# The GRU gates of a graph layer as seven block products of 384 columns instead of 256, with two products added in place

## The chip, the cores and the metric

The kernel runs on one core of a Trainium2 chip. The metric is the device time of one execution in microseconds (us), taken as the median of several runs. A separate profiled execution gives the trace from which all durations of instructions come. The engines are named as in the profile: PE is TensorE (matmul), PEld its weight load, DVE VectorE, ACT ScalarE, POOL GpSimd, SP SyncE (which here only issues DMAs).

## The reference

64 graphs of 256 nodes with 256 features go through two layers, each followed by a residual and a LayerNorm. Layer 0 is a normalised adjacency product and a linear layer. Layer 1 has a convolution over the nodes with 17 taps (branch `x_conv`), a message branch (`x_nmp`), and then a GRU cell, which is what the change touches:

```python
x_in = jnp.concatenate([x_conv, x_nmp], axis=-1)
gi = x_in @ w_ih.T + b_ih
gh = x @ w_hh.T + b_hh
r = jax.nn.sigmoid(gi_r + gh_r)
z = jax.nn.sigmoid(gi_z + gh_z)
nn_ = jnp.tanh(gi_n + r * gh_n)
return (1.0 - z) * nn_ + z * x
...
x = _layernorm(x + _L1_gnn_ref(...), axis=-1)
```

`gi` has 768 columns (r, z, n) from 512 inputs, `gh` 768 columns from 256. r and z need only the sum of both parts; n needs its two parts apart, because r multiplies one of them. Everything is fp32.

## The kernel before

**Stages.** The 64 graphs are taken in four quarters of 16 (`Q`, `NQ`). `graphs` (L960) makes layer 0 and the first pieces of layer 1 for a graph; its result for the gates goes out to memory as `xn` (x transposed, and the message branch). The convolution is done in the frequency domain for a whole quarter at once: `products` (L557) multiplies by the transformed weights in twelve steps, `complex_end` (L731) transforms back on VectorE and writes `xc_d`. Then `gru` (L832) computes the gates of one graph. The main loop (L1056) mixes these generators:

- four graphs of each of the first three quarters have their gates early, among the layer pieces of the last graphs of the next quarter (`gates(q, range(EARLY))`, L1094);
- the other twelve wait (`late`, L1101) and are mixed with the next quarter's `products` and then with its `complex_end`; `paced` (L942) hands out pieces of `complex_end` at a rate per marked VectorE operation of the gates (`mark`, L91; `RATES`, L1042);
- in the last quarter the late gates of the third lie beside `complex_end` alone (L1086), and its own 16 graphs of gates stand at the end with nothing beside them (L1103).

**Order.** Program order is made by these generators (each `yield` is a place where another may put a piece in). When the kernel is built, a planner fixes one order for each engine, by program order among the instructions that it expects to be ready. On the chip each engine executes its fixed order.

**Banks.** Matmul results of `products` and of `gru` go to four PSUM banks (`accbank`, L85), used in turn; a bank is given out again when its last reader is done. Each holds 512 fp32 columns.

**The gates of a graph.** `inputs` holds six chunks of 128 input rows by 256 nodes: chunks 0 and 1 are x, 2 and 3 the message branch, 4 and 5 the convolution branch, which `transposed` (L800) puts there. r and z are made from a 2 by 2 blocking: three chunks by three, 128 nodes by 128 nodes (`halves`, L818), and r columns by z columns. In Strassen's way (Winograd's form) seven block products take the place of eight. Their left sides are A11, A12, A22 and four sums S made by GpSimd (`input_sums`, L822), their right sides B11, B21, B22 and four differences T of weights, made once (L997). Each block product is three matmuls of 256 columns (`block`, L844); `first` (L859), L860, L865, L866 and L869 put the seven together on VectorE, L868 and L870 make tanh of half the value (sigmoid).

n is then made directly: for each half of the nodes six matmuls of 256 columns, two for the x part and four for the rest, into the two halves of one bank (L883). L888 to L908 add the bias, multiply by r, add, take tanh, and mix with x. LayerNorm (L313) and an output DMA follow, on `x1_g`, of which there are two buffers.

A trace shows each fp32 matmul as two PE records, so a graph has 42 records in L846 and 24 in L883.

Of the kernel before, what the change touches and what calls it, by code (L numbers as in the profile page):

```python
# [14 lines left out]
P = 128  # L15
# [11 lines left out]
def kernel(  # L27
# [93 lines left out]
    vectors = const.tile([16, P], F32, name="bn_in")  # L121
# [29 lines left out]
    wrz = const.tile([P, 7, HALF, D], F32)  # L151
    B11, B21, B22, T1, T2, T3, T4 = range(7)
    wn = const.tile([P, 3 * DCH, D], F32)
    brz_t = const.tile([P, 2, D], F32)
    bn_t = const.tile([P, 2, D], F32)
# [266 lines left out]
    def x1_transposed(g):  # L422
        x1 = X1.pop(g)
        xn = XN[g] = work.tile([P, 2 * DCH, N], F32, name="xn")
        p = bank("p_x1T").rearrange("p (k n) -> p k n", k=DCH)
        for k in range(DCH):
            for c in range(NCH):
                nc.tensor.transpose(p[:, k, c * P : (c + 1) * P], x1[:, c, k * P : (k + 1) * P], ident)
        nc.scalar.copy(xn[:, :DCH], p)  # L429

    def layer1(g, place):
# [4 lines left out]
        x1T = xn[:, :DCH]  # L436
# [80 lines left out]
        nc.scalar.copy(xn[:, DCH:], p)  # L517
# [115 lines left out]
    def turned(re, im, angle):  # L633


        t = freq.tile([P, 2, D], F32, name="turn", bufs=3)
        x, y = M[:, re, :], M[:, im, :]
        real_part(t[:, int(re > im), :], x, y, angle)
        return imaginary_part(t[:, int(re < im), :], x, y, angle), t
# [4 lines left out]
    def real_transform():  # L644


        sub2(M[:, 0:3:2, :], M[:, 1:4:2, :])
        yield

        sub2(M[:, 4:6, :].rearrange("p a o -> p (a o)"), M[:, 6:8, :].rearrange("p a o -> p (a o)"))  # L650
        add2(M[:, 6, :], M[:, 7, :])
        r = math.sqrt(0.5)
        for i, by in enumerate((-1.0, 1.0, -r, r)):
            stt(M[:, 4 + i, :], M[:, 4 + i, :], by, M[:, i, :], op0=ALU.mult, op1=ALU.add)
        stt(M[:, 0:4, :], M[:, 0:4, :], 2.0, M[:, 4:8, :], op0=ALU.mult, op1=ALU.subtract)
        yield

        run(four(8, 12))
        yield
        nc.vector.tensor_sub(M[:, 8, :], M[:, 0, :], M[:, 8, :])  # L660
        nc.vector.tensor_add(M[:, 12, :], M[:, 4, :], M[:, 12, :])
        for i, x, y in ((1, 9, 13), (2, 10, 14), (3, 15, 11)):
            angle = math.pi * ORDER[i] / 8
            t = freq.tile([P, 2, D], F32, name="turn", bufs=3)
            by = real_part(t[:, 0, :], M[:, x, :], M[:, y, :], angle)
            imaginary_part(t[:, 1, :], M[:, x, :], M[:, y, :], angle)
            stt(M[:, 8 + i, :], t[:, 0, :], -by, M[:, i, :], op0=ALU.mult, op1=ALU.add)
            stt(M[:, 12 + i, :], t[:, 1, :], by, M[:, 4 + i, :], op0=ALU.mult, op1=ALU.add)
            yield
        stt(M[:, 0:8, :], M[:, 0:8, :], 2.0, M[:, 8:16, :], op0=ALU.mult, op1=ALU.subtract)  # L670
        yield
# [43 lines left out]
    def output(q, n, re, im):  # L715
# [4 lines left out]
        t = freq.tile([P, 2, D], F32, name="turn", bufs=3)  # L720
# [79 lines left out]
    def transposed(g):  # L800
# [3 lines left out]
        if in_blocks(g):  # L804
            behind(nc.vector.transpose(xcT.rearrange("p k (s r) -> p k s r", r=RB), CONV.pop(g)))
            nc.gpsimd.tensor_tensor(xcT, xcT, inputs[:, :DCH], op=ALU.add)
            for k in range(DCH):
                nc.scalar.activation(xcT[:, k], xcT[:, k], AF.Relu, bias=bn2_bias[:, k : k + 1])  # L808
            return
# [12 lines left out]
    def input_sums(g):  # L822
        A11, A12, A21, A22 = halves(GATE[g][1])
        S = SUMS[g] = gate.tile([P, 4, HALF, P], F32, name="sums", bufs=1)
        nc.gpsimd.tensor_tensor(S[:, 0], A21, A22, op=ALU.add)  # L825
        second = nc.gpsimd.tensor_tensor(S[:, 1], S[:, 0], A11, op=ALU.subtract)  # L826

        with tc.issue_after(second.ins):
            nc.gpsimd.tensor_tensor(S[:, 2], A11, A21, op=ALU.subtract)
            nc.gpsimd.tensor_tensor(S[:, 3], A12, S[:, 1], op=ALU.subtract)  # L830

    def gru(g):  # L832
# [5 lines left out]
        trz = gate.tile([P, 4, D], F32, name="trz", bufs=1)  # L838
        nn = gate.tile([P, NCH, D], F32, name="nn", bufs=1)
# [4 lines left out]
        def block(p, j, a, b):  # L844
            for k in range(HALF):
                nc.tensor.matmul(  # L846
                    p[:, j * D : (j + 1) * D], a[:, k], wrz[:, b, k], start=k == 0, stop=k == HALF - 1
                )

        p15, p26 = accbank("p_rz"), accbank("p_rz")  # L850
        block(p15, 0, A11, B11)
        block(p26, 0, A12, B21)
        block(p15, 1, S[:, 0], T1)
        block(p26, 1, S[:, 1], T2)
# [3 lines left out]
        first = gate.tile([P, 2, D], F32, name="first", tag="gn")  # L858
        mark(nc.vector.tensor_add(first, half(p15), brz_t), 1)  # L859
        nc.vector.tensor_add(trz[:, 0:2], first[:, 0:1].to_broadcast([P, 2, D]), half(p26))  # L860
        p7, p34 = accbank("p_rz"), accbank("p_rz")
        block(p7, 0, S[:, 2], T3)
        block(p34, 0, S[:, 3], B22)
        block(p34, 1, A22, T4)
        nc.vector.tensor_add(trz[:, 3], trz[:, 1], p7[:, :D])  # L865
        mark(nc.vector.tensor_add(trz[:, 1:3], trz[:, 1:4:2], half(p34)), 1)  # L866

        nc.scalar.activation(trz[:, 0:4:2], trz[:, 0:4:2], AF.Tanh, scale=0.5)  # L868
        nc.vector.tensor_add(trz[:, 1:4:2], trz[:, 1:4:2], first[:, 1:2].to_broadcast([P, 2, D]))  # L869
        nc.scalar.activation(trz[:, 1:4:2], trz[:, 1:4:2], AF.Tanh, scale=0.5)  # L870
# [3 lines left out]
        for c in range(NCH):  # L874
            terms = [(inputs[:, k, c * P : (c + 1) * P], wn[:, k]) for k in range(3 * DCH)]
            if c == 0 and following:
                input_sums(g + 1)
            if c == 1 and g % Q + 2 < Q:
                load_conv(g + 2)
            p = accbank("p_n")  # L880
            for o, part in ((1, terms[:DCH]), (0, terms[DCH:])):
                for j, (lhsT, w) in enumerate(part):
                    nc.tensor.matmul(  # L883
                        p[:, o * D : (o + 1) * D], lhsT, w, start=j == 0, stop=j == len(part) - 1
                    )

            gn = gate.tile([P, 2, D], F32, name="gn")
            mark(nc.vector.tensor_add(gn, p.rearrange("p (i d) -> p i d", i=2), bn_t), 1)  # L888
            nc.vector.scalar_tensor_tensor(
                gn[:, 1, :], trz[:, 2 * c], 1.0, gn[:, 1, :], op0=ALU.add, op1=ALU.mult  # L890
            )
            nc.vector.scalar_tensor_tensor(  # L892
                gn[:, 0, :], gn[:, 1, :], 0.5, gn[:, 0, :], op0=ALU.mult, op1=ALU.add
            )
            nc.scalar.activation(nn[:, c, :], gn[:, 0, :], AF.Tanh)  # L895


            if g == B - 1:
                part = slice(c, c + 1)
            elif c == NCH - 1:  # L900
                part = slice(0, NCH)
            else:
                yield
                continue
            y, t, n = x1[:, part], trz[:, 1:4:2][:, part], nn[:, part]
            mark(nc.vector.scalar_tensor_tensor(y, t, 3.0, y, op0=ALU.add, op1=ALU.mult), 1)
            nc.vector.scalar_tensor_tensor(n, t, 1.0, n, op0=ALU.subtract, op1=ALU.mult)
            nc.vector.tensor_sub(y, y, n)  # L908
            layernorm(y, nc.scalar, 4 * LN_EPS)
            nc.scalar.dma_start(out[g].rearrange("(c p) d -> p c d", p=P)[:, part], y)  # L910
            yield
# [61 lines left out]
    with tc.tile_pool(name="setup", bufs=1) as setup:  # L973
# [10 lines left out]
        def gate_weights():  # L984
            for b, half_inputs, cols in ((B11, 0, 0), (T1, 0, 1), (B21, 1, 0), (B22, 1, 1)):
                at = slice(cols * D, (cols + 1) * D)
                if half_inputs == 0:
                    parts = ((slice(0, DCH), w_hhT), (slice(DCH, HALF), w_ihT[D : D + P]))
                else:
                    parts = ((slice(0, 1), w_ihT[D + P :]), (slice(1, HALF), w_ihT[:D]))  # L990
                for k, w in parts:
                    nc.sync.dma_start(wrz[:, b, k], w[:, at].rearrange("(k p) o -> p k o", p=P))
            for k, w in ((0, w_hhT), (DCH, w_ihT[D:]), (2 * DCH, w_ihT[:D])):
                nc.sync.dma_start(wn[:, k : k + DCH], w[:, 2 * D :].rearrange("(k p) o -> p k o", p=P))
            yield

            for to, a, b in ((T3, B22, T1), (T1, T1, B11), (T2, B22, T1), (T4, B21, T2)):  # L997
                with tc.issue_after(marks[-1][0]):
                    nc.vector.tensor_sub(wrz[:, to], wrz[:, a], wrz[:, b])
# [10 lines left out]
        brz = brz_t.rearrange("p i d -> p (i d)")  # L1010
        nc.vector.tensor_add(brz, bih_t[:, : 2 * D], bhh_t[:, : 2 * D])
        nc.vector.tensor_sub(brz_t[:, 1], brz_t[:, 1], brz_t[:, 0])
        nc.vector.tensor_copy(bn_t[:, 0, :], bih_t[:, 2 * D :])
        nc.vector.tensor_copy(bn_t[:, 1, :], bhh_t[:, 2 * D :])
# [143 lines left out]
```

## Time and profile before

| what | value |
|---|---|
| median of 3 runs | 2149.64 us (2147.59 to 2150.93) |
| the profiled execution, first to last instruction | 2152.3 us |
| granted TensorE clock, mean | 0.990 of full |
| PE records in L883 (n) | 1536, 355.1 us busy |
| PE records in L846 (r, z) | 2688, 348.6 + 271.6 us busy |
| VectorE at L859 to L869 (5 operations a graph) | 42.9 + 43.6 + 26.5 + 43.9 + 64.6 us |
| VectorE at L888, L889, L892 (twice a graph) | 87.3 + 69.9 + 69.8 us |
| GpSimd at L825 to L830 (4 sums a graph) | 67.1 + 72.6 + 79.6 + 79.9 us |

The span of the profiled execution lies 2.7 us above the median of the runs. Busy time of PE is the union of its records; records overlap (each lasts about 380 ns, one starts every 216 ns), so a sum of durations says nothing.

### The profile page before, as it was taken

What the parts mean: (1) busy time and instruction counts of PE and PEld (TensorE: products, weight loads), DVE (VectorE), ACT (ScalarE), POOL (GpSimd) and SP (SyncE); (2) the same over time, 40 slices, a digit from 0 to 9 for tenths busy, and PEclk for the clock granted to TensorE, in tenths of its full rate; (3) what the DMA queues carried; (4) which work ended last, traced back from release to release, by engine and by line L of the source; (5) the groups of instructions that cost most, each with busy time, mean ns of one, the idle gap of its engine ahead of it and who ended that gap; (6) DMA issues with size and microseconds to landing.
All of it is one profiled execution on the core that took longest, in us unless ns stands there. A gap on an engine that the chain in (4) does not pass through costs nothing.

```text
span 2152.3 us, 28977 instructions
## 1 busy us (share of the span) xinstructions
PE 2052.7 (95%) x9693; PEld 1735.8 (81%) x9693; DVE 1581.6 (73%) x3719; ACT 841.9 (39%) x1857; POOL 664.8 (31%) x640
## 2 busy tenths in 40 slices
PE   7999999887999999899999999999999998999997
PEld 5888788776888888788888888777888887788886
DVE  5555578775568788775656988876566889988887
ACT  4665643456431123445552122446553112222222
POOL 2444310121431244213322133323231123444442
PEclk9999999999999999999999999999999999999999
DMA  4766666434346644233326654324324744443331
GB/s 122 235 196 197 198 194 207 142 132 134 96 146 203 203 110 128 93 112 113 113 94 190 205 157 113 118 98 133 102 88 136 243 116 122 119 102 99 94 84 54
DMA packets 295085, 298.30 MB, mean 139 GB/s; under 512 B 76414, under 2 KB 273618, under 8 KB 294938
## 3 DMA queue, kind: packets, MB, share of 16 engines
q1 hardware_dynamic: 235050, 200.46, 30.9%
q10 hardware_dynamic: 44480, 67.39, 8.8%
q0 software_dynamic: 15408, 28.61, 6.1%
q8 instruction: 77, 1.26, 0.2%
q14 instruction: 70, 0.57, 0.1%
HBM read 193.28 MB, written 103.06 MB: 138 GB/s over the span
## 4 chain that ended last, share of the span: by engine, by line
PE 44%; DVE 12%; issue 9%; POOL 6%; ACT 4%; DMA 2%; ACTq 0%; SPq 0%; POOLq 0%; DVEq 0%
PE p_rz L846 14%; PE p_n L883 8%; PE p_k L539 7%; PE p_out L409 2%; PE p_nmp L513 2%; PE p_hT L399 2%; PE p_dft L480 2%; POOL ln_rs L323 2%; PE p_conv L443 1%; PE p_msg L464 1%; PE p_dist L504 1%; POOL sums L826 1%; POOL sums L825 1%; DMA u<-ud 1%; POOL xc_g L796 1%
## 5 line engine op out<-in xcount | busy, mean ns | idle before, releaser
L883 PE MATMUL p_n<-wn,inputs 128*128 128x256 f32 x1536 | 355.1, 385 | 13.4 <-DVE first L859 13.2
L846 PE MATMUL p_rz<-wrz,sums 128*128 128x256 f32 x1536 | 348.6, 380 | 1.3 <-DVE gn L888 0.8
L883 PEld LDWEIGHTS p_n<-wn,inputs 128*128 128x128 f32 x1536 | 288.5, 192 | 64.2 <-DVE first L859 20.9
L846 PEld LDWEIGHTS p_rz<-wrz,sums 128*128 128x128 f32 x1536 | 290.0, 190 | 44.5 <-issue 5.2
L846 PE MATMUL p_rz<-wrz,inputs 128*128 128x256 f32 x1152 | 271.6, 379 | 1.0 <-ACT inputs L808 1.0
L323 POOL TENSOR_TENSOR ln_rs<-ln_rs,neg_half 128x2 f32<-128x2 f32 x129 | 99.1, 768 | 510.9 <-DVE ln_rs L322 464.0
L846 PEld LDWEIGHTS p_rz<-wrz,inputs 128*128 128x128 f32 x1152 | 217.6, 190 | 31.1 <-ACT inputs L808 1.2
L895 ACT ACTIVATE nn<-gn 128x256 f32<-128x256 f32 x128 | 53.3, 417 | 332.1 <-DVE gn L892 331.7
L539 PE MATMUL p_k<-u,VM 128*128 128x256 f32 x736 | 175.2, 380 | 2.7 <-DMA u<-ud 1.9
L369 POOL TENSOR_TENSOR dis<-deg,neg_half 128x2 f32<-128x2 f32 x64 | 46.1, 720 | 423.6 <-DVE deg L367 393.1
L333 ACT ACTIVATE x_g<-x_g,ln_mr,ln_rs 128x256 f32<-128x256 f32 x128 | 70.0, 593 | 241.5 <-DVE ln_mr L331 241.5
L539 PEld LDWEIGHTS p_k<-u,VM 128*128 128x128 f32 x736 | 138.1, 190 | 24.4 <-DMA u<-ud 4.1
L480 PE MATMUL p_dft<-fwd,h 128*128 128x240 f32 x512 | 120.2, 379 | 25.9 <-ACT h L447 24.6
L399 PE MATMUL p_hT<-adjT,x 128*128 128x256 f32 x512 | 129.8, 397 | 14.0 <-DVE adjT L381 7.6
L825 POOL TENSOR_TENSOR sums<-inputs 128x384 f32<-128x384 f32 x64 | 67.1, 1048 | 239.0 <-ACT inputs L816 206.3
L480 PEld LDWEIGHTS p_dft<-fwd,h 128*128 128x128 f32 x512 | 95.2, 192 | 47.6 <-ACT h L447 41.2
L506 DVE TENSOR_TENSOR aT<-aT,adjT 128x512 f32<-128x512 f32 x64 | 44.6, 698 | 118.2 <-ACT aT L505 118.1
L443 PE MATMUL p_conv<-wc,xn 128*128 128x259 f32 x512 | 125.8, 388 | 4.3 <-ACT xn L429 4.3
L392 POOL TENSOR_TENSOR x_t<-x_t,b_t 128x512 f32<-128x512 f32 x64 | 85.4, 1334 | 142.6 <-ACT x L391 97.4
L409 PE MATMUL p_out<-w,hT 128*128 128x256 f32 x512 | 123.1, 383 | 1.4 <-ACT hT L404 0.7
L464 PE MATMUL p_msg<-wmsg,xn 128*128 128x256 f32 x512 | 121.4, 380 | 0.0
L513 PE MATMUL p_nmp<-aT,msg 128*128 128x256 f32 x512 | 121.2, 379 | 0.2 <-DVE aT L506 0.2
(157 smaller groups left out, 3910.2 us busy)
## 6 DMA issues: line engine op xcount, KB each, us to landing
u<-ud SPq DMA_DIRECT2D x284, 256.0 KB
xn_d<-xn ACTq DMA_DIRECT2D x64, 512.0 KB
inputs<-xn_d SPq DMA_DIRECT2D x64, 512.0 KB
ud<-u_set POOLq DMA_DIRECT2D x39, 480.0 KB, 6.1
adj_t<-in_adj_dram SPq DMA_DIRECT2D x64, 256.0 KB
x_t<-in_x_dram SPq DMA_DIRECT2D x64, 256.0 KB
x_d<-x ACTq DMA_DIRECT2D x64, 256.0 KB
xc_d<-VM SPq DMA_DIRECT2D x64, 256.0 KB
```

The costliest lines, as they stand in the source:

```text
L323: nc.gpsimd.tensor_tensor(rs[:, : len(chunks)], rs[:, : len(chunks)], neg_half[:, : len(chunks)], op=ALU.pow)
L392: nc.gpsimd.tensor_tensor(x_t, x_t, b0_t.unsqueeze(1).to_broadcast([P, NCH, D]), op=ALU.add)
L399: nc.tensor.matmul(p[:, k, :], x1[:, mc, k * P : (k + 1) * P], adjT[:, mc, 1 - mc : 3 - mc, :].rearrange("p n q -> p (n q)"), start=mc == ...
L409: nc.tensor.matmul(p[:, c, :], hT[:, k, c * P : (c + 1) * P], w0[:, k, :], start=k == 0, stop=k == DCH - 1)
L443: nc.tensor.matmul(p, x1T[:, k, c * P : (c + 1) * P], wc1[:, k, :], start=k == 0, stop=k == DCH - 1)
L464: nc.tensor.matmul(p[:, c, :], x1T[:, k, c * P : (c + 1) * P], wmsg[:, k, :], start=k == 0, stop=k == DCH - 1)
L480: nc.tensor.matmul(p[:, t0 * FL : t1 * FL], h[:, c, k * P : (k + 1) * P], fwd[:, first : first + t1 - t0, :].rearrange("p t f -> p (t f)") ...
L513: nc.tensor.matmul(p[:, k, :], msg[:, mc, k * P : (k + 1) * P], aT[:, mc].rearrange("p n q -> p (n q)"), start=mc == 0, stop=mc == NCH - 1,)
L539: nc.tensor.matmul(p[:, j * D : (j + 1) * D], v[:, k, :], u[:, k, :], start=k == 0, stop=k == DCH - 1)
L825: nc.gpsimd.tensor_tensor(S[:, 0], A21, A22, op=ALU.add)
L846: nc.tensor.matmul(p[:, j * D : (j + 1) * D], a[:, k], wrz[:, b, k], start=k == 0, stop=k == HALF - 1)
L883: nc.tensor.matmul(p[:, o * D : (o + 1) * D], lhsT, w, start=j == 0, stop=j == len(part) - 1)
```

## The change

All of r, z, and both parts of n go through the seven block products. The output columns are split in halves of 128 (`HD`) instead of in r and z, and each half has four kinds of columns: n from x (`GN`), r, z, and n from the other inputs (`GI`), 512 columns in one bank. The input chunks are reordered so that each half of the inputs has one chunk of x and two others. The x chunk feeds GN, GR and GZ, the other two chunks GR, GZ and GI, so each matmul has 384 columns, and one block product (three matmuls) fills one bank. Two of the seven products, S3·B22 and A22·T4, are added by TensorE onto the banks of S0·T1 (`p5`) and S2·T3 (`p7`) after VectorE has read those for another sum; VectorE then reads the banks again. `G` takes the place of `trz`, `nn`, `gn` and `first`. One sum (the bias of the second column half) is made by GpSimd. The last elementwise steps work on all 512 values of a kind at once.

```diff
+    ball = const.tile([P, 2, 4, D // 2], F32)
+    vectors = ball[:16, 0, 0, :]
...
-    wrz = const.tile([P, 7, HALF, D], F32)
+    HD = D // 2
+    GN, GR, GZ, GI = range(4)
+    wall = const.tile([P, 7, HALF, 3, HD], F32)
-    wn = const.tile([P, 3 * DCH, D], F32)
-    brz_t = const.tile([P, 2, D], F32)
-    bn_t = const.tile([P, 2, D], F32)
...
-        nc.scalar.copy(xn[:, :DCH], p)
+        nc.scalar.copy(xn[:, 0 : 2 * DCH : 2 * DCH - 1], p)
...
-        nc.scalar.copy(xn[:, DCH:], p)
+        nc.scalar.copy(xn[:, 1 : 1 + DCH], p)
...
-        t = freq.tile([P, 2, D], F32, name="turn", bufs=3)
+        t = freq.tile([P, 2, D], F32, name="turn", bufs=2)
...
+    def input_sums(g, which=(0, 1, 2, 3)):
         A11, A12, A21, A22 = halves(GATE[g][1])
-        S = SUMS[g] = gate.tile([P, 4, HALF, P], F32, name="sums", bufs=1)
...
+        S = SUMS.setdefault(g, [])
+        for i in which:
+            S.append(gate.tile([P, HALF, P], F32, name=f"sums{i}", bufs=1))
+            x, y, op = ((A21, A22, ALU.add), (S[0], A11, ALU.subtract), (A11, A21, ALU.subtract), (A12, S[1 % len(S)], ALU.subtract))[i]
+            nc.gpsimd.tensor_tensor(S[i], x, y, op=op)
...
+        G = gate.tile([P, NCH, 2, 4, HD], F32, name="G", bufs=1)
...
+        def product(a, b, p=None):
+            first = p is None
+            if first:
+                p = accbank("p_g")
             for k in range(HALF):
                 nc.tensor.matmul(
+                    p[:, : 3 * HD] if k == 0 else p[:, HD:], a[:, k], wall[:, b, k].rearrange("p t d -> p (t d)"),
+                    start=first and k == 0, stop=True, skip_group_check=not first or k > 0,
+                )
+            return p
...
+        p1 = product(A11, B11)
+        p2 = product(A12, B21)
+        p6 = product(S[1], T2)
         yield
         if following:
             sent(g + 1)
+        mark(nc.vector.tensor_add(quarter(0, 0), p1, bias(0)), 1)
+        nc.vector.tensor_add(quarter(1, 0), quarter(0, 0), p6)
+        nc.gpsimd.tensor_tensor(quarter(0, 1), quarter(1, 0), bias(1), op=ALU.add)
+        nc.vector.tensor_add(quarter(0, 0), quarter(0, 0), p2)
+        p5 = product(S[0], T1)
+        p7 = product(S[2], T3)
+        mark(nc.vector.tensor_add(quarter(1, 1), quarter(0, 1), p5), 1)
         if following:
             transposed(g + 1)
         yield
+        product(S[3], B22, p5)
+        mark(nc.vector.tensor_add(quarter(1, 1), quarter(1, 1), p7), 1)
+        if following:
+            input_sums(g + 1)
+        yield
+        product(A22, T4, p7)
+        nc.vector.tensor_add(quarter(0, 1), quarter(0, 1), p5)
+        mark(nc.vector.tensor_add(quarter(1, 0), quarter(1, 0), p7), 1)
...
+            nc.scalar.activation(
+                both[:, :, GR : GZ + 1, :].rearrange("p q t d -> p q (t d)"),
+                both[:, :, GR : GZ + 1, :].rearrange("p q t d -> p q (t d)"), AF.Tanh, scale=0.5,
             )
+            nc.vector.scalar_tensor_tensor(n, r, 1.0, n, op0=ALU.add, op1=ALU.mult)
+            nc.vector.scalar_tensor_tensor(i, n, 0.5, i, op0=ALU.mult, op1=ALU.add)
+            nc.scalar.activation(i, i, AF.Tanh)
...
+            mark(nc.vector.scalar_tensor_tensor(yq, z, 3.0, yq, op0=ALU.add, op1=ALU.mult), 1)
+            nc.vector.scalar_tensor_tensor(i, z, 1.0, i, op0=ALU.subtract, op1=ALU.mult)
+            nc.vector.tensor_sub(yq, yq, i)
```

In the text below q00, q10, q01 and q11 are the four quarters of `G` (node half, column half), with the operation that writes them named after them. The weights are loaded by 16 DMAs in place of 11 (rows of 128 columns in place of 256), and the four differences of weights are 1152 columns wide instead of 768.

## The prediction

> **What bounds the kernel now.** I read the page first, then busy time by stage, then the timeline of TensorE and VectorE in two stages, then the waits. In these windows the columns are length, PE, PEld, DVE, ACT and POOL busy us (with instructions), granted clock, DMA share and GB/s.
>
> ```profile
> PE 2052.7 (95%) x9693; PEld 1735.8 (81%) x9693; DVE 1581.6 (73%) x3719; ACT 841.9 (39%) x1857; POOL 664.8 (31%) x640
> ...
> 536.00:642.00 106.00, 102.25 (x486) 86.73 (x484) 64.80 (x164) 43.26 (x96) 43.87 (x42) 1.00 0.40 117
> 642.00:755.00 113.00, 112.57 (x530) 99.02 (x531) 90.70 (x169) 19.73 (x39) 22.99 (x21) 1.00 0.69 206
> 755.00:960.00 205.00, 194.55 (x916) 163.94 (x915) 168.38 (x397) 78.77 (x175) 63.80 (x60) 0.98 0.38 111
> 960.00:1148.00 188.00, 185.46 (x905) 155.57 (x904) 112.69 (x302) 100.59 (x232) 61.25 (x62) 1.00 0.36 108
> ...
> 1740.00:1905.00 165.00, 153.66 (x710) 132.01 (x709) 155.79 (x322) 37.68 (x79) 66.55 (x58) 0.99 0.43 117
> 1905.00:2152.00 247.00, 235.86 (x1080) 203.96 (x1080) 201.51 (x363) 69.66 (x136) 102.46 (x98) 0.99 0.30 83
> ```
>
> TensorE is 95% busy overall, but the stages differ. From the starts of `first` (L859, once per graph) and the program, the 64 gate graphs fall into five kinds of place. A: 12 lie among layer-0 and layer-1 pieces (536:642, 960:1148, 1470:1655), TensorE full, VectorE near 60%. B: 10 lie among the convolution's products (642:755 and its two repeats), TensorE full, VectorE about 80%. C: 16 lie beside `complex_end` and layer pieces (755:960, 1265:1470), TensorE 95%. D: 10 lie in 1740:1905 beside `complex_end` alone, where VectorE (94%) is the bound and TensorE waits for it. E: the last 16 stand alone.
>
> ```profile
> 2005.95 5.45 PE L883 MATMUL p_n<-wn,inputs 128*128 128x256 f32 x24
> 2011.23 2.75 PE L846 MATMUL p_rz<-wrz,inputs 128*128 128x256 f32 x12
> 2013.82 5.34 PE L846 MATMUL p_rz<-wrz,sums 128*128 128x256 f32 x24
> 2019.00 1.46 PE L846 MATMUL p_rz<-wrz,inputs 128*128 128x256 f32 x6
> 2020.35 5.45 PE L883 MATMUL p_n<-wn,inputs 128*128 128x256 f32 x24
> ```
>
> This is one graph of E on TensorE (start, length, then the group): 14.40 us from one p_n to the next, 66 records (each fp32 matmul leaves two), no hole. VectorE in the same time:
>
> ```profile
> 2011.81 0.71 DVE L906 SCALAR_TENSOR_TENSOR x_g<-trz,x_g 128x512 f32<-128x512 f32 x1 [0.70 <-ACT trz L870]
> ...
> 2016.51 1.60 DVE L907 SCALAR_TENSOR_TENSOR nn<-trz,nn 128x512 f32<-128x512 f32 x1 [0.48 <-ACT nn L895]
> 2018.15 0.69 DVE L908 TENSOR_TENSOR x_g<-x_g,nn 128x512 f32<-128x512 f32 x1
> 2018.88 0.75 DVE L320 BATCH_NORM_STATS2 ln_st<-x_g 128x6 f32<-128x256 f32 x2
> 2019.55 0.17 DVE L321 BATCH_NORM_AGGREGATE ln_mv<-ln_st 128x2 f32<-128x6 f32 x1
> 2019.63 0.66 DVE L859 TENSOR_TENSOR first<-p_rz,brz_t 128x512 f32<-128x512 f32 x1
> ```
>
> VectorE never waits for TensorE here. `first` at 2019.63 reads a bank that was full by about 15.1, so VectorE runs 4 us behind, and p_n at 2020.35 starts just after it: both engines go round in 14.4 us. TensorE is allowed that lag because the four accbank banks lie between them.
>
> **What the Trainium skill says.** "TensorE: Matmul & The Clock Gate", Back-to-back issue gap: N/2.4 + 2.5 ns per matmul. The trace agrees: 24 records of 256 columns from 2013.82 to 2019.00 are 215.8 ns each (the formula's 215.8), 8 of 240 columns in p_dft took 1118.10 to 1119.72, 202.5 each. So 384 columns are 322.5, an estimate. "SBUF — State Buffer", Who interferes with whom: a VectorE instruction with two SBUF inputs contends with GpSimd, one with a single SBUF input doesn't. The trace agrees: L907 took 1.60 instead of 0.69 while POOL's L806 ran (2016.31 to 2017.58), and L888, which reads PSUM, averages 682 ns and hardly moves. "PSUM — Partial Sum Buffer", PSUM bank collisions: engines have to be kept apart by bank with semaphores. So TensorE can add to a bank only after VectorE's read; the nearest wait in the trace is p_n on `first` (13.2 us of PE idle).
>
> **The change, part by part.**
>
> TensorE: 66 records of 256 columns become 42 of 384, 42 x 322.5 = 13.55 us. Before, each p_n batch of 24 took 5.28 instead of 5.18 and the A22 batch 1.35 instead of 1.29, some 0.16 a graph at bank changes and waits; I keep 0.15. That is 13.7 against 14.4: 0.7 us less a graph where TensorE binds, 45 us at most over 64.
>
> VectorE: starts of independent operations lie 0.60 us apart at 512 elements and 0.34 at 256 (1801.26 to 1801.86, 1802.46 to 1802.79), a dependent one follows after 0.72. Before, nine operations of 512 and five of 256: 9 x 0.60 + 5 x 0.34 = 7.1. After, seven PSUM adds and five SBUF operations, all of 512: 7.2. VectorE gets no relief. ScalarE: four tanh (2 x 0.63 + 2 x 0.42) become one of 1024 (from 0.42 and 0.63: 1.06) and one of 512; it is idle enough not to matter except as latency. GpSimd gets one add of 128x512 a graph, 1.3 us (L806, L392).
>
> The new waits: S3·B22 may start only when VectorE has read p5 (q11), which waits for POOL's add, which waits for q10, which waits for product p6. Behind the waiting matmul stands all of TensorE's later work in its fixed order. G has one buffer, so the next graph's first add waits for this graph's last read.
>
> E, the loop that this closes: q00 0.72, q10 0.72, POOL 1.27 + 0.07, q11 0.74, two products on TensorE 12 x 0.3225 + 0.16 for the last to land = 4.03, q10 again 0.73, tanh 1.12, n and i 1.44, tanh 0.69, i and subtraction 1.44, the two bn_stats and an aggregate that come ahead (2018.88 to 2019.63) 0.75: 13.7. One of the five SBUF operations meeting a POOL sum adds about 0.9 (as L907). So 14.6, and 0.1 for a matmul already begun: 14.7 for 14.40. Bounds: 13.7 (TensorE's own) to 15.5. 16 x 0.3 = +4.8.
>
> D: 16.5 us a graph, VectorE-bound. It gains 0.1 of work, and POOL's 1.3 us lies beside SBUF-only `complex_end` operations that then run at about half speed: +0.5; and 0.1 for the loop. Bounds 0 to +1.5. 10 x 0.7 = +7.
>
> A: p5's read is 4 us and a layer piece away from its second product, so the wait is covered: 12 x -0.7 = -8.4. Without cover it would be E's.
>
> B: 10 x -0.7 = -7. But p5 and p7 stay in their banks across two product steps, which leaves two of four for p_k1, p_k0, p_k2: the third waits for ScalarE's copy of the second (L580, 0.58, about 0.8 with its signals). Twice a graph, half of it filled by the gate's own matmuls: +0.8. Net +1.0. Bounds: -7 to +9.
>
> C: half of 0.7 is worth having at 95% busy, -5.6; the wait for q11 less well covered, +0.4 a graph, +6.4. Net +0.8. Bounds -11 to +12.
>
> Rest: the last graph has no work to cover its wait, and its tail gains a tanh before n: +0.8. Weights come in 512 byte rows by 16 DMAs on SP's queue instead of 11 with 1 KB, ahead of later loads, but at 72 to 93 us, long before use; L999's four subtractions grow by half (3.7 us in all before): +1.2 together, bounds 0 to 5. `turn` with two buffers is written and read by VectorE alone: nothing. The new place of x1T and of the sums moves addresses only; four sums tiles free POOL a little earlier: nothing. SP's `inputs` loads still wait behind x_g, which waits for an output DMA (143 us in the last stage); I leave that unchanged, its cost is in the upper bounds.
>
> Sum: -8.4 + 1.0 + 0.8 + 7 + 4.8 + 2 = +7.2, so 2159.5 for 2152.3. The median of the runs is 2.7 under the profiled span: 2157.
>
> **Rivals.**
>
> *Covered (faster).* The planner moves the next graph's p1 or a product ahead of the waiting matmul, VectorE's lag shrinks for want of anything to lag behind, and TensorE's saving holds: A -8.4, B -7, C -8, D and E 0, rest +2: -21, 2131, as a median 2128. For it: A to C hold 38 graphs at 95 to 99% TensorE. Against: C's VectorE is 82% busy and D's 94%. It decides if E's period is below 14.4 and B shows no new wait.
>
> *Round trip (much slower).* VectorE's lag of some 4 us, harmless today, becomes TensorE's wait in B to E, 0.8 a graph net over 52 graphs: +42 - 8 + 2 = +35, 2185. For it: `first` is late by 4 us in E, and TensorE already waits 1.4 to 2.4 for it in D. Against: the planner orders by what it expects ready. That a 384-column record costs 343 ns and the change saves TensorE nothing (14.4/42) would end near here, at 2178.
>
> *Balance.* The gains of A to C and the losses of D and E cancel: 2150.
>
> **How the numbers follow.** Forecast 0.43, covered 0.30, round trip 0.15, balance 0.12. A measurement here tells 0.2% (4.3 us) from no change. Faster is the covered case and a little of balance, 0.32; the same is most of balance and the forecast's lower edge, 0.13; slower 0.55. The forecast's own range is 2150 to 2168; with the bounds of both other cases, 2127 to 2187.
>
> **What would show it.** Right: records of 384 columns about 322 ns apart; E's period 14.5 to 14.9 with holes in TensorE before the second p5 product, put down to VectorE; D's VectorE fuller than 94% at 17 us a graph; A shorter by some 3 us per stretch of four. Wrong: no wait of TensorE on q11 and E at 13.7 to 14.2 (covered); or waits over 1 us a graph in B and C (round trip).

## The result and the profile after

The changed kernel takes 2210.24 us (median of 4 runs, 2207.61 to 2213.74) beside 2148.61 us for the kernel before (4 runs, 2146.57 to 2150.93): 1.029 times, with an interval of 1.0272 to 1.0308. The profiled execution has a span of 2205.8 us, 53.5 more than before. The forecast of 2157 had the direction right and the size wrong by 53 us.

The parts of the span show at once that the loss lies in one place. The places are bounded by the starts of each graph's first add (L859 before, L864 after; graphs are counted from 1 here, while `g` in the code counts from 0), by the last p_k matmul and by the end:

```
                                        before             after     difference  forecast
start to the last p_k matmul (A, B, C)  1737.9            1730.1        -7.8      -5.4
from there to graph 48 (D)               166.5             174.8        +8.3      +7
graph 48 to graph 64 (E)                 229.2             281.3       +52.1      +4.8
graph 64 to the end                       18.7              19.7        +1.0      +0.8
```

First the page of the kernel after, and its busy time in two windows, E the second of them (columns as in the prediction's windows):

```profile
PE 2021.5 (92%) x8157; PEld 1442.6 (65%) x8157; DVE 1556.9 (71%) x3593; ACT 821.7 (37%) x1731; POOL 724.4 (33%) x704
...
1730.00:1905.00 175.00, 150.06 (x468) 85.22 (x466) 155.65 (x302) 34.65 (x58) 70.78 (x67) 0.98 0.41 109
1905.00:2187.00 282.00, 229.62 (x674) 127.41 (x673) 181.79 (x306) 58.99 (x96) 114.65 (x112) 0.98 0.27 71
```

In E no engine is full: TensorE is busy 229.6 of 282 us (81%), VectorE 64%. Before, TensorE had 235.86 of 247 there. So no single engine's work fills E, and what holds it has to be sought in the waits. One graph of E on TensorE in the timeline (start, length, group, and in brackets the idle time ahead of it):

```profile
2065.49 2.17 PE L846 MATMUL p_g<-wall,sums 128*128 128x384 f32 x6 [1.30 <-DVE ln_mv L321]
2067.50 0.81 PE L846 MATMUL p_g<-wall,inputs 128*128 128x384 f32 x2
2070.11 2.17 PE L846 MATMUL p_g<-wall,sums 128*128 128x384 f32 x6 [1.80 <-DVE G L870]
2072.12 5.32 PE L846 MATMUL p_g<-wall,inputs 128*128 128x384 f32 x16
2077.28 4.03 PE L846 MATMUL p_g<-wall,sums 128*128 128x384 f32 x12
```

The two holes are 3.1 us of a period of 16.8. The second one, ahead of S3·B22, waits for the add of q11 (L870), the wait that the prediction had named. The first, ahead of S2·T3 (`p7`), is put down to L321, which ran just after the graph's first add (L864, 2064.69); more likely it is the wait for the bank of p1, which that add frees. Sixteen records from 2055.00 to 2060.16 are 322.5 ns each, so the change saves TensorE what it should. The same graph on VectorE, ScalarE and GpSimd, from q10 to the subtraction that frees `G`:

```profile
2065.45 0.69 DVE L865 TENSOR_TENSOR G<-G,p_g 128x512 f32<-128x512 f32 x1
...
2065.50 0.99 POOL L828 TENSOR_TENSOR sums<-sums,inputs 128x384 f32<-128x384 f32 x1
2066.05 0.46 DVE L322 TENSOR_SCALAR ln_rs<-ln_mv 128x2 f32<-128x2 f32 x1
2066.43 0.67 DVE L867 TENSOR_TENSOR G<-G,p_g 128x512 f32<-128x512 f32 x1
2066.45 1.27 POOL L866 TENSOR_TENSOR G<-G,ball 128x512 f32<-128x512 f32 x1
...
2067.68 0.70 POOL L323 TENSOR_TENSOR ln_rs<-ln_rs,neg_half 128x2 f32<-128x2 f32 x1
2068.35 0.99 POOL L828 TENSOR_TENSOR sums<-inputs 128x384 f32<-128x384 f32 x1
2068.42 0.95 DVE L331 SCALAR_TENSOR_TENSOR ln_mr<-ln_mv,ln_rs 128x2 f32<-128x2 f32 x1 [1.31 <-POOL ln_rs L323]
2069.29 0.68 DVE L870 TENSOR_TENSOR G<-G,p_g 128x512 f32<-128x512 f32 x1
...
2076.07 0.69 DVE L892 SCALAR_TENSOR_TENSOR G<-G 128x512 f32<-128x512 f32 x1 [0.50 <-ACT G L888]
2076.68 0.68 DVE L897 SCALAR_TENSOR_TENSOR x_g<-G,x_g 128x512 f32<-128x512 f32 x1
...
2077.28 0.69 DVE L893 SCALAR_TENSOR_TENSOR G<-G 128x512 f32<-128x512 f32 x1
...
2078.00 0.63 ACT L894 ACTIVATE G<-G 128x512 f32<-128x512 f32 x1 [1.96 <-DVE G L893]
2078.19 1.27 POOL L806 TENSOR_TENSOR inputs<-inputs 128x512 f32<-128x512 f32 x1 [4.75 <-DMA inputs<-xn_d]
2078.66 1.35 DVE L898 SCALAR_TENSOR_TENSOR G<-G 128x512 f32<-128x512 f32 x1 [0.70 <-ACT G L894]
...
2080.04 0.69 DVE L899 TENSOR_TENSOR x_g<-x_g,G 128x512 f32<-128x512 f32 x1
```

This is the loop of the prediction with strangers in it. GpSimd starts q01 at 2066.45, when its sum for the next graph is through. q01 ends at 2067.72, and q11 could start; but VectorE's order has L331, the last step of the LayerNorm of the graph *before*, ahead of q11. L331 waits for GpSimd's power (L323), which stands behind q01, and then takes 0.95 us for 2 elements per partition while a GpSimd sum runs. q11 starts at 2069.29, 1.57 us after q01 ended (0.03 where nothing stands between, as a timeline below shows). Further down, y (L897) stands between the two steps of n: L893 starts 1.21 us after L892, where the sum had 0.72. And L898 is stretched from 0.69 to 1.35 beside GpSimd's L806. q01 itself starts 0.31 us after q10 ended, where the sum had 0.07. Together 0.24 + 1.54 + 0.49 + 0.66 = 2.9 us of the 3.1 by which this period exceeds the sum of 13.7; the other links agree with the sum to 0.2 us in all.

Three of the sixteen periods are longer still, 19.9 to 20.8 us: there GpSimd's first two sums wait for the next graph's inputs, and q01 waits behind them. In these three TensorE's hole ahead of S3·B22 is 3.5 to 3.8 us long, and from about its end the granted clock is at half for 3.4 us, which it is nowhere else in the sixteen (the clock is the third figure from the end):

```profile
1911.97:1915.38 3.41, 3.09 (x5) 1.85 (x6) 0.86 (x2) 0.70 (x2) 0.00 (x0) 0.50 0.23 77
2017.79:2021.19 3.40, 3.40 (x7) 1.73 (x6) 0.44 (x2) 0.00 (x0) 0.32 (x1) 0.50 0.27 86
2123.60:2127.00 3.40, 3.40 (x7) 1.74 (x6) 0.69 (x1) 0.00 (x0) 0.99 (x1) 0.50 0.35 123
```

The waits of the stage from 1905 to 2187 (total us, times, longest):

```profile
PEld p_g L846 <- POOL sums L828: 58.9, 23, 4.4
PE p_g L846 <- DVE G L870: 36.1, 16, 3.8
...
DVE ln_mr L331 <- POOL ln_rs L323: 27.4, 16, 3.6
...
PE p_g L846 <- DVE ln_mv L321: 16.3, 17, 1.4
```

The wait on q11 comes in each of the 16 graphs, 2.3 us on the mean, and the wait of L331 for the power in each too. Before the change L331 took 0.95 us in all 16 graphs of E as well (one of them below), and TensorE had no hole of 1.5 us or more there; that fits the lag of VectorE that the prediction read, which leaves TensorE time to spare.

```profile
2021.98 0.95 DVE L331 SCALAR_TENSOR_TENSOR ln_mr<-ln_mv,ln_rs 128x2 f32<-128x2 f32 x1 [0.82 <-POOL ln_rs L323]
```

The first row of the waits counts weight loads, which run ahead of the matmuls, so it isn't TensorE's lost time.

### The profile page after: what moved, and what is told of

The parts are those of the page before. It is cut to its first block, busy times and chain, and to the rows that moved or that the text cites. A ratio compares the mean times of both kernels' runs of the same rounds, so it can differ in the third digit from the quotient of the medians.

```text
span 2205.8 us, 25754 instructions
## 1 busy us (share of the span) xinstructions
PE 2021.5 (92%) x8157; PEld 1442.6 (65%) x8157; DVE 1556.9 (71%) x3593; ACT 821.7 (37%) x1731; POOL 724.4 (33%) x704
## 4 chain that ended last, share of the span: by engine, by line
PE 41%; DVE 18%; POOL 6%; DMA 4%; issue 3%; ACT 3%; SPq 0%; POOLq 0%; DVEq 0%; ACTq 0%
PE p_g L846 22%; PE p_k L539 5%; PE p_hT L399 2%; PE p_nmp L513 2%; PE p_dft L480 2%; PE p_out L409 2%; PE p_conv L443 2%; POOL sums L828 2%; POOL ln_rs L323 2%; PE p_msg L464 2%; DMA inputs<-xn_d 1%; POOL G L866 1%; DMA u<-ud 1%; DVE VM L588 1%; DVE G L870 1%
## 5 line engine op out<-in xcount | busy, mean ns | idle before, releaser
L846 PE MATMUL p_g<-wall,sums 128*128 128x384 f32 x1536 | 542.6, 496 | 93.2 <-DVE G L870 61.2
L846 PEld LDWEIGHTS p_g<-wall,sums 128*128 128x128 f32 x1536 | 284.8, 191 | 306.2 <-POOL sums L828 78.8
L846 PE MATMUL p_g<-wall,inputs 128*128 128x384 f32 x1152 | 402.7, 493 | 10.9 <-DVE G L875 10.1
L846 PEld LDWEIGHTS p_g<-wall,inputs 128*128 128x128 f32 x1152 | 218.6, 193 | 157.6 <-DVE G L875 14.4
L828 POOL TENSOR_TENSOR sums<-inputs 128x384 f32<-128x384 f32 x128 | 137.0, 1071 | 234.0 <-PE p_g L846 170.1
L323 POOL TENSOR_TENSOR ln_rs<-ln_rs,neg_half 128x2 f32<-128x2 f32 x129 | 98.9, 767 | 344.2 <-DVE ln_rs L322 292.6
L369 POOL TENSOR_TENSOR dis<-deg,neg_half 128x2 f32<-128x2 f32 x64 | 45.7, 714 | 328.8 <-DVE deg L367 325.6
L331 DVE SCALAR_TENSOR_TENSOR ln_mr<-ln_mv,ln_rs 128x2 f32<-128x2 f32 x129 | 57.3, 444 | 117.1 <-POOL ln_rs L323 116.4
L888 ACT ACTIVATE G<-G 128x1024 f32<-128x1024 f32 (+1 forms) x65 | 67.9, 1044 | 185.5 <-DVE G L881 182.3
L866 POOL TENSOR_TENSOR G<-G,ball 128x512 f32<-128x512 f32 x64 | 81.7, 1277 | 112.5 <-DVE G L865 65.1
```

Source lines behind the costliest of these rows:

```text
L323: nc.gpsimd.tensor_tensor(rs[:, : len(chunks)], rs[:, : len(chunks)], neg_half[:, : len(chunks)], op=ALU.pow)
L828: nc.gpsimd.tensor_tensor(S[i], x, y, op=op)
L846: nc.tensor.matmul(p[:, : 3 * HD] if k == 0 else p[:, HD:], a[:, k], wall[:, b, k].rearrange("p t d -> p (t d)"), start=first and k == 0, ...
L866: nc.gpsimd.tensor_tensor(quarter(0, 1), quarter(1, 0), bias(1), op=ALU.add)
```

## The experiments

Two questions were open: is it the loop that holds E, or TensorE itself; and which of the strangers costs what. Below, "E" is the mean period from graph 50 to 63 and "D" that from graph 39 to 48 in the profiled execution. Before: E 14.40, D 16.39. After: E 17.46, D 17.17. The stage is compared, not the total alone: up to graph 36 the engines of six of these runs have the instructions of the kernel after in the same order, and yet graph 36 started between 1617.7 and 1628.2 us (1618.5 after). Each E and D is that of one execution, and in two runs (two buffers in the last 16 graphs, and the last step of the order) it was the fastest of five.

The granted clock has to be read beside D. In the runs with own banks, with two buffers from graph 37 on, with q01 on VectorE in all graphs and with the sums behind q01, D was 17.87 to 18.91 us and the clock there 0.93 to 0.94; in all the others, before and after among them, D was 16.39 to 17.33 and the clock 0.99 or more. In E it was 0.98 or more everywhere. Whether a lower clock made D longer, or longer waits of TensorE came first, no run separates.

**Own banks.** S3·B22 and A22·T4 get banks of their own, and VectorE adds p5 and p7 a second time (two more adds of a graph). This takes TensorE's wait on q11 out.

```
-        product(S[3], B22, p5)
+        nc.vector.tensor_add(quarter(0, 1), quarter(0, 1), p5)
+        p3 = product(S[3], B22)
...
-        product(A22, T4, p7)
+        nc.vector.tensor_add(quarter(1, 0), quarter(1, 0), p7)
+        p4 = product(A22, T4)
```

> Edit: S3*B22 and A22*T4 get banks of their own, p5 and p7 are read twice by VectorE at once, so there are nine PSUM adds instead of seven and no TensorE add in place. Theory P: TensorE is free again, a graph of the last stage returns to 14.3 to 14.6, total 2160 to 2170. Theory L: only the 4.1 us of the two products leave the loop and about 2.5 us of adds come in, a graph of the last stage takes 15.5 to 16, and beside complex_end VectorE's 1.2 us more cost 10 us: total 2185 to 2195.

Measured: 2159.84 us, 1.0054 (1.0032 to 1.0076); E 14.27, D 18.11. Two adds more on VectorE, and 50 us less: TensorE's records of 384 columns, equally many as after, run at 14.27 us per graph, so TensorE isn't what holds E after. The expectation had put 15.5 to 16 us on this run for the loop, and that missed; the other theory, by which the adds in place are what costs, had 14.3 to 14.6.

**Two buffers for the quarters**, in place adds kept; the second lies in memory that is free by then, from graph 37 on (`g` = 36) in the first run and in the last 16 graphs in the second:

```
-        G = gate.tile([P, NCH, 2, 4, HD], F32, name="G", bufs=1)
+        if g < B - Q:
+            G = gate.tile([P, NCH, 2, 4, HD], F32, name="G", bufs=1)
+        else:
+            room = V2.rearrange("p f k n -> p (f k n)")
+            G = room[:, g % 2 * 2048 : (g % 2 + 1) * 2048].rearrange("p (c h t d) -> p c h t d", c=NCH, h=2, t=4)
```

> Edit: from graph 36 on, G alternates between two places (in V2's memory, which is free by then), everything else as it is. Theory L: the loop opens, since the next graph's first sums no longer wait for this graph's last read; a graph of the last stage takes 13.8 to 14.6 us instead of 17.4, total 2150 to 2165. Theory P: TensorE still waits for q11 in each graph; a graph of the last stage stays at 16.5 or more, total at 2190 or more.

> Two buffers for the quarters in the last 16 graphs alone (the earlier run had them from graph 36 on). Loop theory: 14.5 to 14.9 us per graph in the last stage, as in that run; graphs 38 to 48 as in the changed kernel, 17.2 us each; 2162 to 2170 us. Rival, the slower 18.2 us per graph beside complex_end that the earlier run showed was not due to its second buffer: 18 us there again and 2174 to 2180 us.

Measured: 2176.84 us, 1.0131 (1.0102 to 1.0161), E 14.66, D 18.23; and 2166.94 us, 1.0101 (1.0077 to 1.0126), E 14.47, D 16.90. The slower D of the first run is not there where D keeps its one buffer; the clock in D was 0.93 in the first and 1.00 in the second, and why isn't settled. E falls by 3 us in both. So the loop needs both links, the one buffer and the adds in place; cut either and it is open.

**GpSimd's q01 on VectorE**, in all graphs:

```
-        nc.gpsimd.tensor_tensor(quarter(0, 1), quarter(1, 0), bias(1), op=ALU.add)
+        nc.vector.tensor_add(quarter(0, 1), quarter(1, 0), bias(1))
```

> Edit: the add that makes the bias sum q01 goes from GpSimd to VectorE, nothing else. Theory L (a closed loop through the single G buffer, lengthened by GpSimd's turn and by the fixed orders around it): in the last stage the way from q10 to q11 falls from 3.8 us to about 1.5, so a graph takes 14.7 to 15.2 us instead of 17.4, and the total is 2165 to 2175. Theory P (TensorE's two adds in place, which have to wait for VectorE, are what costs): q11 is still a VectorE read ahead of TensorE, a graph stays at 16.8 or more, the total at 2198 or more. Beside complex_end (VectorE-bound) both expect some 0.6 us a graph more from the added VectorE operation, less what GpSimd no longer blocks.

Measured: 2196.98 us, 1.0225 (1.0181 to 1.0270); E 16.09, D 17.87. E gains 1.4 us, less than the forecast for it. It lies between the two theories' numbers and decided nothing by itself, but its trace shows a second way round the loop. TensorE's wait on q11 is nearly gone (3.5 us in 5 graphs of E, 36.1 in 16 after), and what is left is the hole ahead of S2·T3:

```profile
PE p_g L846 <- DVE ln_mv L321: 26.1, 16, 1.9
...
2063.60 2.17 PE L846 MATMUL p_g<-wall,sums 128*128 128x384 f32 x6 [1.76 <-DVE ln_mv L321]
...
2065.61 1.45 PE L846 MATMUL p_g<-wall,inputs 128*128 128x384 f32 x4
...
2067.07 2.17 PE L846 MATMUL p_g<-wall,sums 128*128 128x384 f32 x6
```

S2·T3 starts when the first add (q00) is done, and S3·B22 stands behind it and behind four records of the next graph's first product in TensorE's order (two in the kernel after). From S2·T3 to S3·B22 that is 3.47 us, and q11 (L870, at 2066.24 in this graph) was done before it.

**GpSimd's sums behind q01**: the four sums of the next graph may not be issued before q01.

```
-        nc.gpsimd.tensor_tensor(quarter(0, 1), quarter(1, 0), bias(1), op=ALU.add)
+        q01 = nc.gpsimd.tensor_tensor(quarter(0, 1), quarter(1, 0), bias(1), op=ALU.add)
...
-            input_sums(g + 1)
+            with tc.issue_after(q01.ins):
+                input_sums(g + 1)
```

> Edit: GpSimd's four sums for the next graph are held behind this graph's q01 in its order. Theory L: q01 starts at once after q10 (0.3 us a graph sooner) and the graphs of 19 to 21 us in the last stage, in which q01 stands behind two sums that wait for a late load, come down to 17: total 2192 to 2200. Theory P: no change, 2203 to 2209, or a loss where the sums come too late for the products.

Measured: 2222.48 us, 1.0344 (1.0305 to 1.0383); E 16.86, D 18.91. A miss: E gains 0.6, but D loses 1.7, and graph 48 starts 26 us later than after. The clock in D was 0.94 here; the cause of the loss in D is open.

**L331 behind q11**: the first of four steps that take the strangers out of the loop one by one, each on top of the one before and in the last 16 graphs alone, with one buffer and the adds in place as after. The rest of the LayerNorm (L331, ScalarE's scaling, the output's DMA) is held until q11 of the next graph has been issued; x1 has three places in free memory meanwhile.

```
         mark(nc.vector.tensor_add(quarter(1, 1), quarter(0, 1), p5), 1)
+        while LATER:
+            LATER.pop(0)()
...
-            layernorm(y, nc.scalar, 4 * LN_EPS)
+            layernorm(y, nc.scalar, 4 * LN_EPS, LATER if held else None)
```

> In the last 16 graphs the last VectorE step of the LayerNorm of the previous graph (L331, which waits for GpSimd's power) moves from ahead of the add of quarter (1,1) (L870) to behind it; nothing else moves in VectorE's or GpSimd's order. Theory of the loop with fixed orders: this wait is about 1.5 us in every period of the loop between the four quarters in one buffer, so a graph of the last stage takes 15.8 to 16.3 us in place of 17.46, and the kernel 2184 to 2192 us in place of 2210. Rival, TensorE itself (the accumulation onto banks already read, a lower granted clock) holds the stage: L870 comes earlier but the period stays at 17.2 to 17.5, and the time within 4 us of 2210.

Measured: 2197.83 us, 1.0235 (1.0209 to 1.0261); E 16.36, just short of the 15.8 to 16.3 (and 2184 to 2192 us) expected, and far from the rival's 17.2. In E the order of GpSimd's instructions is that of the kernel after, and on VectorE one instruction of a graph has moved: 1.1 us a graph. The third place for x1 came with it and wasn't tried alone; the load of x1 still waited for an output's DMA (159.0 us in 13 graphs of the last stage, 199.5 in 16 after). Most periods now come in turns, 14.6 to 14.8 us and 17.4 to 19.3. The timeline of a long one (L838, L876, L880 here are L828, L866, L870 after; q11 follows q01 by 0.03 us):

```profile
2100.13 0.91 ACT L818 ACTIVATE inputs<-inputs,bn_bias 128x256 f32<-128x256 f32 x2 [2.61 <-POOL inputs L816]
...
2101.17 1.00 POOL L838 TENSOR_TENSOR sums<-inputs 128x384 f32<-128x384 f32 x1 [1.07 <-ACT inputs L818]
...
2102.24 0.99 POOL L838 TENSOR_TENSOR sums<-sums,inputs 128x384 f32<-128x384 f32 x1
2103.20 1.26 POOL L876 TENSOR_TENSOR G<-G,ball 128x512 f32<-128x512 f32 x1
...
2104.49 0.69 DVE L880 TENSOR_TENSOR G<-G,p_g 128x512 f32<-128x512 f32 x1 [2.56 <-POOL G L876]
```

q01 (L876) stands behind two sums that wait for ScalarE and, through it, for the next graph's inputs. q10 started at 2100.52; q01 could have started near 2101.2, and started 2 us later.

**And q01 on VectorE**, so that no GpSimd instruction stands ahead of q11:

```
-        nc.gpsimd.tensor_tensor(quarter(0, 1), quarter(1, 0), bias(1), op=ALU.add)
+        on = nc.gpsimd if g < B - Q else nc.vector
+        on.tensor_tensor(quarter(0, 1), quarter(1, 0), bias(1), op=ALU.add)
```

> On top of e9_norm_behind, the add of quarter (0,1) goes from GpSimd to VectorE in the last 16 graphs, so that no GpSimd instruction stands before the add of quarter (1,1) any more. Theory: what e9_norm_behind left over (periods of 17.4 to 19.3 us in turn with periods of 14.7) is quarter (0,1) behind two GpSimd sums that wait for the next graph's inputs; all periods become 14.6 to 15.0 us and the kernel 2164 to 2174 us. Rival: late inputs hold TensorE's third product of the next graph all the same, whoever adds the quarter; the turns of long and short periods stay, mean 16.0 to 16.4 us, 2190 to 2198 us.

Measured: 2184.06 us, 1.0171 (1.0153 to 1.0189); E 15.45. The rival's turns of long and short periods are gone, but the mean is above the 14.6 to 15.0 of the theory, and the total above its 2164 to 2174 us: of the periods from graph 50 on, nine are 14.8 to 15.4 and four 15.8 to 16.8. Not all of the 0.9 us comes from GpSimd's queue: on VectorE the add itself is shorter in the loop, 0.72 in place of 1.27 + 0.07, so some 0.6 of it may be that, as an estimate from the prediction's figures.

**And y behind n**: L897 may not be issued before the step that completes n.

```
-            nc.vector.scalar_tensor_tensor(i, n, 0.5, i, op0=ALU.mult, op1=ALU.add)
+            added = nc.vector.scalar_tensor_tensor(i, n, 0.5, i, op0=ALU.mult, op1=ALU.add)
...
-            mark(nc.vector.scalar_tensor_tensor(yq, z, 3.0, yq, op0=ALU.add, op1=ALU.mult), 1)
+            with tc.issue_after(added.ins) if g >= B - Q else ExitStack():
+                mark(nc.vector.scalar_tensor_tensor(yq, z, 3.0, yq, op0=ALU.add, op1=ALU.mult), 1)
```

> On top of e10_norm_q01, the first blending step on VectorE (y) is put behind the add that completes n, in the last 16 graphs, so that it runs while ScalarE has the second tanh. Theory: its 0.6 us leaves the loop of the quarters: 14.0 to 14.4 us per graph, 9 to 11 us less than e10_norm_q01, with one buffer and the adds in place. Rival: TensorE or the inputs are the bound by then, and nothing changes (within 3 us).

Measured: 2177.76 us, 1.0143 (1.0124 to 1.0161); E 14.85, most periods 14.8. The 0.6 us came, though the total fell by 6.3 us and not by 9 to 11; 14.0 to 14.4 was too low, in part since L331 stood behind q11 but ahead of the read of p7, which A22·T4 needs (L332, L888 here):

```profile
2073.23 0.95 DVE L332 SCALAR_TENSOR_TENSOR ln_mr<-ln_mv,ln_rs 128x2 f32<-128x2 f32 x1 [1.47 <-POOL ln_rs L323]
2074.10 0.67 DVE L888 TENSOR_TENSOR G<-G,p_g 128x512 f32<-128x512 f32 x1
```

**And L331 behind that read too:**

```
-        mark(nc.vector.tensor_add(quarter(1, 1), quarter(1, 1), p7), 1)
+        read = nc.vector.tensor_add(quarter(1, 1), quarter(1, 1), p7)
+        mark(read, 1)
+        with tc.issue_after(read.ins):
+            while LATER:
+                LATER.pop(0)()
```

> On top of e11_norm_q01_y, the last VectorE step of the LayerNorm of the graph before also goes behind VectorE's read of the second bank (the add of p7), since in e11_norm_q01_y it stood before that read, waited 1.47 us for GpSimd's power there, and the read came at 2074.10 where the bank was full about 1.5 us earlier; product A22.T4 has to wait for this read. Theory: this is the last step outside the arithmetic of the loop; 14.0 to 14.3 us per graph in the last 16, as the loop's own sum of 13.7 us plus small losses, 7 to 12 us less in all. Rival: TensorE's wait for the next graph's sums and inputs is the bound by then, and 14.7 to 14.9 us per graph stay.

Measured: 2170.13 us, 1.0105 (1.0085 to 1.0124); E 14.47, above the 14.0 to 14.3 expected, with six of the sixteen periods at 14.30 to 14.31. The timeline of TensorE for one graph:

```profile
2051.57 2.17 PE L856 MATMUL p_g<-wall,sums 128*128 128x384 f32 x6 [0.52 <-DVE ln_mv L321]
2053.58 1.45 PE L856 MATMUL p_g<-wall,inputs 128*128 128x384 f32 x4
2055.02 2.17 PE L856 MATMUL p_g<-wall,sums 128*128 128x384 f32 x6
2057.03 4.68 PE L856 MATMUL p_g<-wall,inputs 128*128 128x384 f32 x14
```

The hole ahead of S3·B22 (at 2055.02) is gone (3 of the 16 graphs still have one, 3.3 us in all), with the same two links that the kernel after has. What is left is the second way round: a hole ahead of S2·T3 (10.6 us over the 16 graphs), then S2·T3 and four records ahead of S3·B22, 3.45 us in all. The four steps took E from 17.46 to 16.36, 15.45, 14.85 and 14.47.

**Own banks but in D**, where the prediction has VectorE as the bound, and then also two buffers for the quarters in the last 16 graphs (the edit above):

```
+        inplace = B - Q - 12 <= g < B - Q
...
+        if not inplace:
+            nc.vector.tensor_add(quarter(0, 1), quarter(0, 1), p5)
+        p3 = product(S[3], B22, p5 if inplace else None)
```

> Own banks for the last two products, and two more VectorE adds, in all graphs but 36 to 47, where TensorE adds in place as in the changed kernel. If VectorE bounds graphs 36 to 47, the two adds of 0.63 us that go from each give back 0.8 to 1.0 us per graph against the run with own banks throughout: 17.2 us per graph there, 14.3 in the last stage, 2148 to 2153 us. Rival, the time there is set by something else (GpSimd, transfers): 18 us as in that run, 2158 to 2162 us.

> As e6_mix, and two buffers for the quarters in the last 16 graphs. If what keeps the last stage at 14.3 us with own banks is still the wait of the first adds for the last read of the quarters of the graph before, 13.6 to 13.9 us per graph and 2141 to 2147 us, which is faster than the kernel before. Rival, TensorE with its holes for GpSimd's sums sets it: 14.2 to 14.4 us per graph, and the time of e6_mix within 3 us.

Measured: 2152.37 us, 1.0025 (1.0014 to 1.0037), E 14.20, D 17.23; and 2143.91 us, 0.9981 (0.9970 to 0.9992), E 13.84, D 16.87. D is 0.88 us shorter than with own banks throughout, as expected if VectorE's two adds count there. But the clock in D was 0.99 here and 0.93 there, so this doesn't show by itself that VectorE's work sets D. The second is faster than the kernel before by 0.2%, the only version here that is. Its window of busy time in E:

```profile
1900.00:2124.00 224.00, 217.84 (x665) 126.02 (x665) 186.84 (x328) 58.35 (x95) 111.82 (x112) 0.99 0.36 89
```

TensorE is busy 217.8 of 224 us (97%): 13.84 a graph is 0.3 above the 13.55 that its 42 records need. What the change saves TensorE is real, once no loop stands in the way.

## Why the prediction was wrong, and where it was right

*Where it failed: E.* The prediction saw the loop and its links, put 13.7 us on it, 0.9 for one collision with GpSimd, and took 14.7. Measured was 17.46 on the mean. The step that failed is that sum: each of its terms is a latency of the arithmetic, added up as if an instruction started when its operands are there. The engines issue in a fixed order, and on VectorE and GpSimd other work stands between the links. GpSimd's sums stood ahead of q01, where the sum had 0.07 us. L331 stood ahead of q11, where it had nothing, and brought in GpSimd's queue a second time through the power. y stood between the steps of n. Taking these out one by one gave back 1.1 us, 0.9 (some of it the shorter add on VectorE), 0.6 and, for L331 ahead of the second read, 0.4. The links that the sum did have were sized right: in the period of 16.8 us shown above they agree with the trace to 0.2 us in all. So the strangers were what was left out; the upper bound should have been taken from what stands in the queues, not from one collision.

The sum also missed the second way round, through the bank of p1 and S2·T3. It doesn't bind in the kernel after, where q11 comes later, but the 14.47 that the four steps reached is its figure and not a confirmation of the 13.7: with 0.81 us from q00 to S2·T3 and 3.45 on to S3·B22 in place of the 3.5 that the sum has from q00 to S3·B22, it comes to about 14.5, an estimate from the last run's timeline.

*The names of the signs.* The prediction said what E would show: holes in TensorE ahead of the second p5 product, put down to VectorE. That came in all 16 graphs, with 2.3 us each.

*D: +7 forecast, +8.3 measured*, 0.78 us more a graph from graph 39 to 48, where 0.7 was put. The sign that was to go with it didn't come: VectorE was busy 155.65 of 175 us (89%), not over 94%, and TensorE waited 11.4 us for q11 there in nine waits. So the size was right and its reason isn't shown: part of the 8.3 may be the loop's, and how it divides wasn't separated. In the five runs whose instructions are those of the kernel after up to graph 48, D was 16.90 to 17.33, so the size stands, to some 0.2 us a graph. GpSimd's add was put at 0.5 of the 0.7; that alone wasn't measured either (with q01 on VectorE D was longer, 17.87, at a clock of 0.94).

*A, B, C: -5.4 forecast, -7.8 measured.* This neither bears the forecast out nor refutes it: in the five runs just named the last p_k matmul started between 1727.7 and 1741.1 us, before the change in its one trace at 1737.9. The sign of A, some 3 us less per stretch of four, can't be read in this either. TensorE waited for q11 only 12.3 us in ten waits from 536 to 1730 us, over 38 graphs: as forecast, the other work covers it.

*TensorE's price* was right, 322.5 ns a record: the 202.5 and 215.8 ns that the prediction read at 240 and 256 columns go on to 322 at 384. The formula of the Trainium skill's "TensorE: Matmul & The Clock Gate", Back-to-back issue gap, doesn't give it as it stands: N/2.4 + 2.5, which the page calls the gap of an isolated matmul, is 109.2 ns for N = 256 and 162.5 for N = 384. The fp32 records of this trace take what the formula gives for twice their columns. *The tail*: +0.8 forecast, +1.0 measured. The setup is part of A.

*The rivals.* The round trip had 2185 us and the right engine, but spread 0.8 us over 52 graphs; what came was 3 us in 16 graphs. "Covered" and "balance" fell with E.

*Contention with GpSimd.* The prediction went by one case, two SBUF inputs. The Trainium skill's "SBUF — State Buffer", section SBUF: two separate sides, names a second, a 2-port perf mode, and calls both an exclusive lock for the whole instruction. L322 has one SBUF input, of 128x2, and took 0.16 us as a rule, but 0.46 beside the sum that ended at 2066.49, and it ended within 0.02 us of it. So an operation with one input can be held too; that it ran in such a mode, the trace doesn't show.

## What to carry to other kernels

When a change turns slack into a loop of waits, don't sum latencies alone: walk through each engine's order between the links, and count every instruction that stands there, with the queues that it waits for in its turn. Small ones count too: an operation on 128x2 elements held a matmul for over a microsecond, because it waited for another engine. And look at the links before the strangers: here a second buffer or separate banks gave E back as much as four moves of the order did together (14.47 and 14.27 us against 14.47), with less work.

## What the runs showed of the hardware

L331, a VectorE operation of 2 elements per partition with two SBUF inputs, takes 0.16 us alone. In the kernel after it started 40 times beside a GpSimd operation of 384 or 512 elements per partition, and each time it ended 0.02 us after that one. In E it took 0.95 us in every graph, since a GpSimd sum always started 0.06 to 0.08 us before it (2068.35 and 2068.42 in the period shown). There its cost was that of the other engine's instruction and not of its own size. It isn't so beside every GpSimd operation: three times it started just after the power of L369 (128x2 elements, 0.70 us), and took 0.16 us.

In the last stages of the kernel after, from 1730 us to graph 64, the granted clock fell to half five times, for 3.4 us each. TensorE had five holes of more than 2.5 us there (2.9 to 3.8), and each fall began within some 1.2 us of the end of one of them. What links the two wasn't tested.
